# Pauses behind GpSimd's gathers: two small scratch writes behind each, of a width set per layer, in place of one behind every second

## The chip, the core and the metric

The kernel runs on one core of a Trainium2 chip. A core has five engines with a queue of instructions each: TensorE (PE in the profile; its weight loads are listed apart as PEld), VectorE (DVE), ScalarE (ACT), GpSimd (POOL) and SyncE (SP), which only issues DMAs. Sixteen DMA engines move data between device memory and the on-chip memories. The metric is the device time of one execution in microseconds (us), lower is better. Three timed runs of the kernel before took 1542.4 to 1545.57 us, with a median of 1544.14 us.

## What is computed

Four graph-attention layers run one after the other over 4096 nodes with 256 features, each as `x = x + layer(relu(layernorm(x)))`. Cut to one head, a layer does:

```python
h = x @ W
s_i, s_j = h @ a1, h @ a2
e = leaky_relu(s_i[:, None] + s_j[None, :], 0.2)
e = where(adj > 0, e, -very_large)
out = softmax(e, axis=1) @ h          # layers 1 and 3: elu of it
```

Layers 0 and 1 have one head; layer 2 has four heads of 64 features; layer 3 forms the softmax of `e` and that of `-e`, both over the same mask. The adjacency matrix `adj` is the same 4096 x 4096 matrix in all layers. Its entry (i, j) is set with a probability that falls with both indices, like `0.0039 * w_i * w_j` with `w_i` proportional to `(1 + i) ** -0.5`: the first rows and columns are rather full, the rest is sparse.

## The kernel before

All of it is `list_layers`. (A dense version, `dense_layers`, stands behind a flag that is set when the lists described here would overflow; with these inputs it is not run.)

**Tiles.** The nodes make 32 tiles of 128. A target tile (whose rows of `x` are being made) is handled by a `Unit`. Dense units take four target tiles at once (512 columns) and go over all 32 source tiles, with features and masks streamed from device memory by SP in chunks of four tiles (`s_gs`, `s_ms`). Listed units take one target tile and go over the four first source tiles (kept on chip, `pre` and `mpre`) and then over a list of only those sources that have an edge into the tile. `DENSE` says how many blocks of four tiles are dense in each layer: 4, 2, 1 and 1; the tiles behind them are listed.

**Lists and gathers.** In layer 0 the kernel builds, for each listed tile, an index (`idx`) of its sources, by VectorE and PE (`list_sources`). Sources come in blocks of 128 rows. `SHARED[T]` blocks hold sources for the whole tile; they are gathered as `s_gg` tiles (six buffers; four in layer 0). `QUADS[T]` groups of four blocks hold sources for one quarter of the tile each; they are gathered as `s_gq` tiles of four parts (two buffers). One gather is one indirect DMA issued by GpSimd: it reads 128 row numbers from `idx` on chip and fetches the 128 rows from a table in device memory (`table`, or `table_own` for the last block in layer 0). The mask of a block is gathered once in layer 0 into `mlist` from `mask_t`, or lies beside the features in the table's row and is copied out of the gathered tile by ScalarE (L1084 and L1174). All gathers go through the helper `gather` (L530), so that in the profile each stands under L532.

By `QUADS` and `SHARED`, layer 0 has 36 + 64 gathers for tiles 16 to 31 and 77 for masks, 177 in all; layer 1 has 69 + 96 for tiles 8 to 31, 165; layers 2 and 3 have 80 + 128 each for tiles 4 to 31, 208.

**The pause.** `gather` counts its calls while the program is built. After every second one (`RUN`) it writes a scratch tile `pause` of 128 x 256 floats with a memset on GpSimd (L541). Nothing reads the tile.

**A step.** For one source block: VectorE forms `p = max(grow, c) * mask` from the target's row factors `grow`, the source's column factor `c` (which lies in the last column of the gathered row) and the mask (L1151; for quads L1107 and L1110; in layer 2 ScalarE does part of it by L1090 and VectorE finishes with L1160). PE multiplies `p` with the source's features into an accumulator (L1193; L1130 for quads; L1210 and L1228 in layer 2). When a unit ends, VectorE and ScalarE normalise and add to `x`, and the pair's rows for the next layer are projected by `node_rows` and `project` (PE L746 and L778) and written to the next layer's table by SP.

**Order.** The order of all work is a written-out plan. `run` goes through it and at each place p issues the fetch of step p (its gathers included), the preparation of step p - 2, the weights of step p - 3 and the matmuls of step p - 6 (`LEAD`), and then a bit of the work that waits in `posts` (unit ends and projections). In layers 1 to 3 the plan begins with some dense steps alone, then listed tiles and dense steps alternate (over 24, 14 and 26 of the tiles), and then come the listed tiles that are left. Layer 1 takes tiles 16 to 31 and then 8 to 15; layers 2 and 3 take tiles 8 to 31 and then 4 to 7. GpSimd's queue keeps the order of the plan (`manual_schedule`); the framework inserts the waits between engines. A gather waits until the last reader of its buffer is done and, in layers 1 to 3, until the rows that it may fetch have been written.

Of the kernel before, what the change touches and what calls it, by code (L numbers as in the profile page):

```python
# [18 lines left out]
P = 128  # L19
# [5 lines left out]
IT = IB // P  # L25
# [454 lines left out]
FRONT = tuple(MW * ((l, False) in MASKS_IN.values()) for l in range(4))  # L480
TW = tuple(FRONT[l] + GW[l] + MW * ((l, True) in MASKS_IN.values()) for l in range(4))
LEAD = (0, 2, 3, 6)
RUN = 2
OWN0 = 7
HW = MW // 2
TURNS = (4, 5, 6, 1, 7, 2, 3)
# [3 lines left out]
def list_layers(ctx: ExitStack, tc: tile.TileContext, a: dict, out: bass.AP, flag):  # L490

    nc = tc.nc
# [32 lines left out]


    pause = const.tile([P, 256], F32, name="pause")
    gathers = [0]

    def gather(dst, src, index_ap, offset):  # L530

        nc.gpsimd.indirect_dma_start(  # L532
            out=dst,
            out_offset=None,
            in_=src,
            in_offset=bass.IndirectOffsetOnAxis(ap=index_ap, axis=0),
            element_offset=offset,
        )
        gathers[0] += 1
        if gathers[0] % RUN == 0:  # L540
            nc.gpsimd.memset(pause, 0.0)  # L541

    x = keep.tile([P, NT, D], F32, name="x")
    mpre = keep.tile([P, DP, N], U8, name="mpre")
    mlist = keep.tile([P, NLIST, P], U8, name="mlist")
# [3 lines left out]
    mask_t = {  # L549
        b: dram.tile([N + 1, IB], U8, name=f"mask_t{b}", tag=f"mask_t{b}")  # L550
        for b in range(NIB)
        if b not in MASKS_IN and b != OWN0
    }
# [139 lines left out]
    def pump(queue, n, width=1, force=False):  # L693

        k = 0
        while n and k < min(width, len(queue)):
            if queue[k][1] > clock[0] and not force:
                k += 1
                continue
            n -= 1  # L700
            try:
                queue[k][1] = clock[0] + (next(queue[k][0]) or 0.0)
            except StopIteration:
                queue.pop(k)

    def ensure(done):
        while not done():
            assert posts
            pump(posts, 1, force=True)
# [272 lines left out]
    index = {}  # L982
# [6 lines left out]
    def mask_slot(T, k):  # L989
        q = QUADS[T]  # L990
        if k >= GR * q:
            return OFFS[T] + k - GR * q, 0, P
        return OFFS[T] + SHARED[T] + k // GR, k % GR * GP, (k % GR + 1) * GP
# [3 lines left out]
    def gather_masks(n, tile=None):  # L997

        for T, k in list(masks_of):
            if not n or tile is None and T not in index:  # L1000
                break
            if tile in (None, T):
                slot, c0, c1 = mask_slot(T, k)
                gather(mlist[:, slot, c0:c1], mask_t[T // IT], index[T][:, k : k + 1], T % IT * P + c0)
                masks_of.remove((T, k))
                n -= 1

# [317 lines left out]
    def run(plan):  # L1325

        n = len(plan)
        for p in range(n + LEAD[3]):
            if p + 4 < n and plan[p + 4][1] == 0 and plan[p + 4][0].is_ready():
                plan[p + 4][0].prepare()  # L1330
            for lead, stage in zip(LEAD, (Unit.fetch, Unit.begin, Unit.weigh, Unit.multiply)):
                if 0 <= p - lead < n:
                    stage(*plan[p - lead])
            if p >= LEAD[3]:
                u = plan[p - LEAD[3]][0]
                clock[0] += u.cost
                pump(posts, u.rates[0], width=2)
                pump(lists_q, u.rates[1])
                gather_masks(u.rates[2])


    def listed_sources(L, T, pool):
        heads = list(range(L.H))
        l, n = L.l, L.part
        at, behind = MASKS_IN.get(T // IT, (-1, False))
        own = at == l
        more = 0 if not own else (T % IT + 1 if behind else IT - T % IT) * MW // IT
        source, first_col = L.table, FRONT[l]
        if T // IT == OWN0:
            at = 0  # L1350
            if l == 0:
                own, behind, source, first_col = True, T % IT >= IT // 2, table_own, HW
                more = (T % IT + 1 - IT // 2 if behind else IT // 2 - T % IT) * MW // IT
        front = 0 if behind else more
        width = GW[l] + more
        c0 = width * 4 - P if behind else 0

        def gather_rows(dst, k):
            gather(dst, source, index[T][:, k : k + 1], first_col - front)

        def get(i):
            if i < DP:
                g = L.g[:, i, :] if l == 0 else L.pre[:, i, :]
                m = mpre[:, i, T * P : (T + 1) * P]
                return heads, [g[:, h * n : (h + 1) * n] for h in heads], m
            ensure(lambda: all(L.ready))
            while T not in index:
                pump(lists_q, 1, force=True)
            if at < 0:
                gather_masks(CAPS[T], T)  # L1370
            k = i - DP
            m = mlist[:, OFFS[T] + k, :]
            if k < SHARED[T]:
                wide = pool.tile([P, width], F32, name=f"s_gg_{l}_{T}_{k}", tag="gg")
                gather_rows(wide, GR * QUADS[T] + k)
                if own:
                    kept, m = m, wide.bitcast(U8)[:, c0 : c0 + P]
                    copies[l, T, i] = kept, m
                g = wide[:, front : front + GW[l]]
                return heads, [g[:, h * n : (h + 1) * n] for h in heads], m  # L1380
            q = k - SHARED[T]
            wide = pool.tile([P, GR, width], F32, name=f"s_gq_{l}_{T}_{q}", tag="gq", bufs=2)
            for a in range(GR):
                gather_rows(wide[:, a, :], q * GR + a)
            if own:
                first = wide.bitcast(U8)[:, :, c0 : c0 + GP]
                rows_at, groups_at, bytes_at = (list(d) for d in first.ap)
                groups_at[0] += GP
                quad_masks[l, T, i] = m.rearrange("p (a i) -> p a i", a=GR), bass.AP(first.tensor, first.offset, [rows_at, groups_at, bytes_at])
            return heads, wide[:, :, front : front + GW[l]], m  # L1390

        return get
# [272 lines left out]
def gat_layers(tc: tile.TileContext, a: dict, out: bass.AP):  # L1665
    nc = tc.nc
    with tc.tile_pool(name="flag", bufs=1) as pool:
        flag = pool.tile([1, 1], I32, name="flag")

        with tc.manual_schedule(engines={mybir.EngineType.Pool}):  # L1670
            list_layers(tc, a, out, flag)
        again = nc.values_load(flag[0:1, 0:1], min_val=0, max_val=1)
        with tc.If(again > 0):
            dense_layers(tc, a, out)
# [45 lines left out]
```

## Time and profile before

| | |
|---|---|
| median of three timed runs | 1544.14 us |
| the profiled execution | 1640.54 us |
| its span, from first to last instruction | 1638.8 us |
| PE busy (matmuls) | 1445.7 us, 88% |
| DVE busy | 1182.5 us, 72% |
| POOL busy | 1037.6 us, 63% |
| ACT busy | 497.3 us, 30% |
| gathers into `s_gq`, 400 | 431.8 us, 1080 ns each |
| gathers into `s_gg`, 258 | 277.2 us, 1074 ns each |
| gathers into `mlist`, 77 | 91.1 us, 1183 ns each |
| `pause`, 379 | 132.3 us, 349 ns each |

The profiled execution is slower than the timed ones because it is recorded; it shows where time goes, not how much a run takes. A row of the groups view reads: line, engine, operation, written tile <- read tiles, shape, count | busy time in us, mean ns of one | idle time of the engine just before, with what ended it. The busy time of a group is the time in which at least one of its instructions ran, so overlapping ones count once. In the windows view each row is a stretch of the span: for each engine the busy time and the number of instructions, then the TensorE clock that was granted (1 is full), the share of time in which the DMA engines were busy, and the traffic. A row of the timeline has start, duration and the idle time in front of the instruction. In the chain of waits each row is a piece of the path that ended last: its start, its length, and the engine, tile and line, or "DMA" with the tiles for the time from a transfer's issue to its landing; "issue" is time for which the profile shows no reason.

### The profile page before, as it was taken

How to read it: one execution, taken by the hardware profiler on the slowest of the kernel's cores; microseconds unless marked ns; L12 is line 12 of the kernel's file. 1: busy time of each engine (PE TensorE's matmuls, PEld its weight loads, DVE VectorE, ACT ScalarE, POOL GpSimd, SP SyncE). 2: the span in 40 equal slices, each digit the busy share in tenths (PEclk: the TensorE clock that was granted, in tenths of full speed). 3: DMA queues.
4: the chain of work that ended last, by engine and by line, in shares of the span. 5: the costliest groups of instructions: out<-in, count | busy, mean ns of one | idle time of the engine just before them, and what ended most of it. 6: DMA issues, size and time to landing. Idle time of an engine off the chain costs nothing.

```text
span 1638.8 us, 30153 instructions
## 1 busy us (share of the span) xinstructions
PE 1445.7 (88%) x10558; PEld 1084.8 (66%) x10558; DVE 1182.5 (72%) x3424; ACT 497.3 (30%) x1569; POOL 1037.6 (63%) x1255
## 2 busy tenths in 40 slices
PE   6999898888888988888989889987877999899995
PEld 4887676666676866666645545566655877688873
DVE  6889989887677467655778879876755466577754
ACT  5631020011112023222335545565744111111111
POOL 9825888883513477767337776555556277867775
PEclk9999999999897999998999999989877999999997
DMA  7899999876414454554323333333333477766665
GB/s 261 283 320 297 320 299 293 223 201 161 115 33 145 112 152 126 141 154 133 114 73 107 97 105 97 106 90 99 91 102 106 131 217 209 217 193 198 205 184 146
DMA packets 161024, 272.72 MB, mean 166 GB/s; under 512 B 29664, under 2 KB 86462, under 8 KB 160862
## 3 DMA queue, kind: packets, MB, share of 16 engines
q1 hardware_dynamic: 117322, 146.32, 28.6%
q0 software_dynamic: 42704, 123.84, 28.2%
q8 instruction: 86, 1.41, 0.4%
q14 instruction: 76, 0.62, 0.1%
q10 hardware_dynamic: 836, 0.53, 0.1%
HBM read 225.22 MB, written 45.39 MB: 165 GB/s over the span
## 4 chain that ended last, share of the span: by engine, by line
PE 49%; DVE 7%; issue 6%; POOL 4%; DMA 4%; ACT 2%; another core or an unknown queue 1%; DVEq 0%; POOLq 0%; ACTq 0%
PE s_acc L1193 26%; PE s_pj L778 6%; PE s_acch L1210 5%; PE s_accm L1228 5%; DVE s_p L1151 3%; POOL s_gq L532 3%; PE s_acc L1130 2%; PE s_sT L1036 2%; DMA s_gq<-table,idx 1%; DMA s_gg<-table,idx 1%; PE s_acch L1130 1%; PE s_tp L746 1%; POOL s_gg L532 1%; DVE s_p L1160 1%
## 5 line engine op out<-in xcount | busy, mean ns | idle before, releaser
L532 POOL DMA_INDIRECT s_gq<-table,idx x400 | 431.8, 1080 | 188.7 <-issue 83.2
L532 POOL DMA_INDIRECT s_gg<-table,idx x258 | 277.2, 1074 | 277.4 <-DVE first L943 55.2
L1193 PE MATMUL s_acc<-g,s_p 128*128 128x257 f32 x1152 | 294.4, 401 | 17.4 <-DVE s_p L1151 12.2
L1193 PEld LDWEIGHTS s_acc<-g,s_p 128*128 128x128 f32 x1152 | 221.0, 200 | 59.7 <-DVE s_p L1151 16.5
L1193 PE MATMUL s_acc<-s_gs,s_p 128*128 128x257 f32 x896 | 212.3, 388 | 1.1 <-issue 0.9
L1151 DVE SCALAR_TENSOR_TENSOR s_p<-s_grow,pre,mpre 128x128 f32<-128x128 f32 (+1 forms) x576 | 188.4, 367 | 28.8 <-PE s_acc L1193 16.3
L778 PE MATMUL s_pj<-s_w,s_hT 128*128 128x259 f32 (+3 forms) x640 | 184.9, 428 | 24.4 <-issue 9.8
L1151 DVE SCALAR_TENSOR_TENSOR s_p<-s_grow,s_gs,s_ms 128x512 f32<-128x512 f32 x224 | 159.6, 748 | 56.5 <-PE s_acc L1193 20.1
L1193 PEld LDWEIGHTS s_acc<-s_gs,s_p 128*128 128x128 f32 x896 | 166.5, 192 | 39.0 <-issue 7.6
L1193 PE MATMUL s_acc<-pre,s_p 128*128 128x257 f32 x768 | 186.3, 391 | 3.2 <-issue 2.2
L1193 PEld LDWEIGHTS s_acc<-pre,s_p 128*128 128x128 f32 x768 | 147.2, 196 | 28.9 <-issue 4.3
L778 PEld LDWEIGHTS s_pj<-s_w,s_hT 128*128 128x128 f32 x640 | 126.2, 208 | 57.8 <-issue 14.4
L1193 PE MATMUL s_acc<-s_gg,s_p 128*128 128x257 f32 x530 | 137.9, 392 | 6.9 <-DVE s_p L1151 3.5
L1151 DVE SCALAR_TENSOR_TENSOR s_p<-s_grow,s_gg,mlist 128x128 f32<-128x128 f32 x363 | 116.5, 344 | 33.6 <-PE s_acc L1193 22.5
L541 POOL MEMSET pause<- 128x256 f32 x379 | 132.3, 349 | 0.2
L532 POOL DMA_INDIRECT mlist<-mask_t,idx x77 | 91.1, 1183 | 65.2 <-DVE idx L978 46.4
L1042 ACT ACTIVATE s_grow<-s_sT 128x256 f32<-128x256 f32 (+2 forms) x136 | 46.9, 368 | 257.4 <-PE s_sT L1036 136.5
L1107 DVE TENSOR_TENSOR s_p<-s_grow,s_gq 128x128 f32<-128x128 f32 (+1 forms) x168 | 52.4, 339 | 97.5 <-DMA s_gq<-table,idx 53.7
L1193 PEld LDWEIGHTS s_acc<-s_gg,s_p 128*128 128x128 f32 x530 | 100.2, 194 | 29.9 <-issue 8.5
L1210 PE MATMUL s_acch<-pre,s_p 128*64 128x65 f32 x1792 | 92.8, 237 | 28.9 <-issue 26.6
L1210 PEld LDWEIGHTS s_acch<-pre,s_p 128*64 128x64 f32 x1792 | 72.3, 144 | 67.0 <-issue 39.3
L1090 ACT ACTIVATE s_p<-s_grow,s_minus,pre 128x128 f32<-128x128 f32 x224 | 96.0, 485 | 62.0 <-PE s_accm L1228 25.7
(154 smaller groups left out, 2077.9 us busy)
## 6 DMA issues: line engine op xcount, KB each, us to landing
s_raw<-in_adjT SPq DMA_DIRECT2D x128, 512.0 KB
s_gs<-table SPq DMA_DIRECT2D x28, 516.0 KB
table<-s_g SPq DMA_DIRECT2D x28, 258.0 KB
mask_t<-s_m SPq DMA_DIRECT2D x28, 256.0 KB
s_ms<-mask_t SPq DMA_DIRECT2D x28, 256.0 KB
s_gq<-table,idx POOLq DMA_INDIRECT x400
table<-s_m SPq DMA_DIRECT2D x21, 256.0 KB
table<-g SPq DMA_DIRECT2D x8, 516.0 KB
```

The lines of the kernel that those rows point to most:

```text
L532: nc.gpsimd.indirect_dma_start(out=dst, out_offset=None, in_=src, in_offset=bass.IndirectOffsetOnAxis(ap=index_ap, axis=0), element_offset ...
L541: nc.gpsimd.memset(pause, 0.0)
L778: nc.tensor.matmul(ps, lhsT=hT[:, c, :], rhs=L.w[:, c, k * (D + 6) : k * (D + 6) + cols], start=(c == 0), stop=(c == 1),)
L1036: nc.tensor.transpose(ps[:, h - h0, it, :], L.s[:, T0 + it, h : h + 1].to_broadcast([P, P]), ident)
L1042: nc.scalar.activation(grow[:, h1:h2, :], ps[:, h1 - h0 : h2 - h0].rearrange("p h a b -> p h (a b)"), AF.Exp, scale=scale,)
L1090: nc.scalar.activation(w[:, h, :], u.grow[:, h, :], AF.Relu, scale=g[h][:, n - 1 : n], bias=minus)
L1107: nc.vector.tensor_tensor(p4[:, h0:h1], grow[:, h0:h1], c[:, h0:h1].to_broadcast([P, h1 - h0, GR, GP]), op=op)
L1130: nc.tensor.matmul(acc, lhsT=p[:, h, part], rhs=g[:, k, h * n : (h + 1) * n - 1], start=False, stop=last, skip_group_check=True,)
L1151: nc.vector.scalar_tensor_tensor(p[:, k, :], u.grow[:, h, :], g[k][:, n - 1 : n], m, op0=ALU.min if L.l == 3 and h == 1 else ALU.max, op1= ...
L1193: nc.tensor.matmul(u.accs[it][h], lhsT=p[:, k, it * P : (it + 1) * P], rhs=g[k][:, 0:n], start=first, stop=last, skip_group_check=u.quads > 0,
L1210: nc.tensor.matmul(u.accs[0][c : c + P // 2, h, :], lhsT=p[:, h, c : c + P // 2], rhs=g[h][:, 0 : DH + 1], start=first and h == 0, stop=la ...
L1228: nc.tensor.matmul(u.accs[h], lhsT=g[k][:, 0 : DH + 1], rhs=p[:, k, :], start=first, stop=last, skip_group_check=True,)
```

## The change

In place of one memset of 256 columns behind every second gather, two memsets stand behind each gather. Both write the same first columns of `pause`; how many is set by the layer of the gather: 176 in layer 0 (its mask gathers too), 144 in layer 1, 256 in layer 2 and 144 in layer 3. `gather` gets the layer as an argument; the counter goes.

```diff
-RUN = 2
+PAUSES = (176, 144, 256, 144)
...
     pause = const.tile([P, 256], F32, name="pause")
-    gathers = [0]
-
-    def gather(dst, src, index_ap, offset):
+
+    def gather(l, dst, src, index_ap, offset):
 
         nc.gpsimd.indirect_dma_start(
...
-        gathers[0] += 1
-        if gathers[0] % RUN == 0:
-            nc.gpsimd.memset(pause, 0.0)
+        for _ in range(2):
+            nc.gpsimd.memset(pause[:, 0 : PAUSES[l]], 0.0)
...
-                gather(mlist[:, slot, c0:c1], mask_t[T // IT], index[T][:, k : k + 1], T % IT * P + c0)
+                gather(0, mlist[:, slot, c0:c1], mask_t[T // IT], index[T][:, k : k + 1], T % IT * P + c0)
...
-            gather(dst, source, index[T][:, k : k + 1], first_col - front)
+            gather(l, dst, source, index[T][:, k : k + 1], first_col - front)
```

## The prediction

> **What bounds the kernel now.** First the cores, then the windows by layer (cut where the tiles' names change layer), the groups with shapes kept apart, POOL's timeline, the chain of waits in order of time. The profiled execution took 1640.54 us (span 1638.8 us and 1.7 us around it); the timed runs have a median of 1544.14 us, 0.94 of it. Sums below are made in profiled time and then multiplied by 0.94. One core runs, so there is no die to compare.
>
> ```profile
> core 0: us, PE busy (x) PEld busy (x) DVE busy (x) ACT busy (x) POOL busy (x), PEclk, DMA share, GB/s
> 0.00:475.00 475.00, 414.20 (x2286) 332.75 (x2287) 392.62 (x992) 113.68 (x413) 321.14 (x383) 0.96 0.81 242
> 475.00:805.00 330.00, 290.90 (x1573) 229.90 (x1572) 204.53 (x618) 82.00 (x293) 193.74 (x248) 0.93 0.47 131
> 805.00:1275.00 470.00, 406.48 (x4827) 256.91 (x4829) 355.79 (x1102) 249.28 (x726) 275.03 (x312) 0.90 0.35 96
> 1275.00:1639.00 364.00, 334.13 (x1884) 265.23 (x1880) 229.53 (x716) 52.33 (x138) 247.64 (x312) 0.97 0.66 190
> ```
>
> PE leads in every layer (86 to 92%). POOL is at 59 to 68%, so on average it is no bound. The chain says otherwise for some stretches; at the end of layer 2:
>
> ```profile
> 1265.29 0.95 POOL s_gq L532
> 1266.24 0.30 issue
> 1266.55 0.95 POOL s_gq L532
> 1267.50 0.00 issue
> 1267.50 0.33 POOL pause L541
> 1267.82 0.17 issue
> 1267.99 1.12 POOL s_gq L532
> 1269.11 0.31 issue
> 1269.42 3.18 DMA s_gq<-table,idx
> ```
>
> Here gathers stand one behind the other on the chain that ends last, each pause too, and the last one's landing (3.18 us from its start) is waited for. Going through the chain piece by piece I count 84 gathers on it: 3 in layer 0, 19 in layer 1, 21 in layer 2, 41 in layer 3. They sit at 685 to 732, 1195 to 1268, 1375 to 1394 and 1583 to 1622 us: where dense work to hide behind has run out, or where heavy tiles (8 or 9 gathers each) come.
>
> **What the skill says.** "Perfetto Trace Analysis", GPSIMD Engine Instruction: the reported span of a GpSimd instruction is unreliable, time them by start-to-start spacing. I do. "SBUF — State Buffer", Who interferes with whom: a VectorE instruction with two SBUF inputs contends with a GpSimd instruction that reads SBUF, not with one that only writes. The trace fits: gathers (which read an index) take 0.95 us at the median but up to 5.02 us, at 908.57 us beside an unbroken run of L1151 steps; the pause has a median of 0.33 us. "TensorE: Matmul & The Clock Gate", Part 1: PE's clock halves after an idle window and needs about 3.4 us of work to come back. The trace fits by its granted clock, 0.937 over the span, 0.90 in layer 2, where PE stalls most.
>
> **The change part by part.** It takes away 379 memsets of 256 columns (one behind every second gather) and a counter that exists only at build time. It adds 2 x 758 = 1516 memsets. By the lists in the code the layers have 177, 165, 208 and 208 gathers (the groups add to the same 758). No DMA, wait or buffer is added or moved.
>
> ```profile
> L541 POOL MEMSET pause<- 128x256 f32 x379 | 132.3, 349 | 0.2
> L507 POOL MEMSET s_ones<- 128x128 f32 x1 | 0.2, 194 | 0.0
> L524 POOL MEMSET places<- 128x1 f32 x28 | 1.0, 98 | 0.0
> ```
>
> ```profile
> 1299.24 1.00 POOL L532 DMA_INDIRECT s_gg<-table,idx  x1 [0.30 <-issue]
> 1300.24 0.33 POOL L541 MEMSET pause<- 128x256 f32 x1
> 1300.73 0.95 POOL L532 DMA_INDIRECT s_gg<-table,idx  x1 [0.17 <-issue]
> 1301.98 0.95 POOL L532 DMA_INDIRECT s_gg<-table,idx  x1 [0.30 <-issue]
> 1302.93 0.33 POOL L541 MEMSET pause<- 128x256 f32 x1
> ```
>
> *Before.* From one gather's end to the next one's start: 0.30 us without a pause, 0.33 + 0.16 = 0.49 us with one. Mean 0.395 us.
>
> *Width.* 128 columns show 194 ns, 256 show 325 ns (the minimum): 1.02 ns a column, 63 ns fixed. So 144, 176 and 256 columns are 210, 243 and 325 ns.
>
> *Two in a row.* The trace has no such pair of this size. The 28 one-column memsets show 98 ns each but fill 1.0 us together, 36 ns each: they overlap by 62 ns. Lower bound of a pair: twice the span less 62 ns; upper bound: twice the span. I take the lower one, as those memsets overlapped throughout.
>
> *After.* Pair plus 0.16 us: 0.52 us at 144, 0.59 at 176, 0.75 at 256 (upper: 0.58, 0.65, 0.81). Added per gather: 0.19 us in layer 0, 0.125 in layers 1 and 3, 0.355 in layer 2. Over all gathers: 34 + 21 + 74 + 26 = 155 us more of POOL (upper 202). No layer comes over 80% of POOL, so most is hidden: by POOL's waits for a free buffer, behind PE's work.
>
> *On the path.* (1) The 84 gathers on the chain: 3 x 0.19 + 19 x 0.125 + 21 x 0.355 + 41 x 0.125 = 15.5 us. (2) Two stretches where POOL's own waits no longer cover it. Counting in POOL's timeline, 712 to 797 us has 55 gathers and 5.7 us of waits against 6.9 us added, and 1298 to 1375 us has 51 gathers and 3.6 us against 6.4 us: 1.2 + 2.8 = 4 us at most, of which I take 3. (3) Layer 0, 140 to 300 us: 98 gathers without one wait, so POOL falls 98 x 0.19 = 18.6 us further behind; from 300 to 460 us it waits 37 us, which takes most of it back. I put 4 us on the path; bounds 0 and 18.6. (4) A gift: a gather held by a VectorE run ends with that run, whenever it was issued. Beyond 0.95 us each (758 x 0.95 = 720 of the groups' 826 us) the gathers spend 106 us, so held; a pause that falls inside is free. I take 4 us off (about a fifth of 1 to 3). Sum: 15.5 + 3 + 4 - 4 = 18.5 us profiled, 17 us timed: 1544 + 17 = 1561, and I say 1560.
>
> *Who is queued behind.* Behind a memset on POOL stand only later gathers (L732 and L736 of layer 0 ended at 92 us, before the first gather). For these wait ScalarE's mask copies (L1084, L1174) and VectorE's L1107, then PE: the copies hold ScalarE's in-order queue, so the next `s_grow` is late too. Late next is the free `s_gq` buffer (two of them), which POOL itself waits for.
>
> **Rivals.** *Faster: layer 0 is short of DMA.* From 140 to 300 us the DMA engines are 97% busy, with the adjacency stream and 98 gathers; slower gathers leave the stream more of it, and their own traffic moves to a stretch at 65%. Price: at most PE's idle time there, 160 - 141.6 = 18 us. It decides if it gives more than the 15 us that the chain costs; then, with the chain's cost half absorbed in held gathers, 1544 - 18 + 7 = 1533. For: the share. Against: VectorE waits only some 5 us for that stream (L1472) from 140 to 460 us. *No change: all is hidden.* POOL idles 600 us of the span; 1544. Against: 84 gathers on the chain. *Much slower: pairs do not overlap and POOL becomes the bound.* Chain 21 us, layer 0 half of 98 x 0.25 = 12, stretches 6, and 8 for PE work at half clock behind stalls grown by some 16 us: 47 x 0.94 = 44, so 1588. For: layer 2's granted clock is already 0.90. *The change doesn't do what it says*: if the second memset, which repeats the first, were dropped on the way to the chip, the gaps would be 0.37 to 0.49 us, close to the 0.395 us of now, and the time with them; this joins the no-change case.
>
> **How the numbers follow.** My forecast 42% (its own range 1550 to 1572), faster by the first rival 37% (1526 to 1540), no change 8%, much slower 13% (1573 to 1595). That gives faster 0.37, same 0.08, slower 0.55; 0.2% is about what a measurement of this kernel can tell from no change. The range 1531 to 1577 leaves out a quarter of the faster case (9%) and most of the last (9%).
>
> **What would show it.** Right: pauses x1516 with spans near 0.21, 0.24 and 0.33 us; gather end to next start 0.52, 0.59, 0.75 us; POOL near 72% busy; more POOL pieces on the chain at the ends of layers 1, 2 and 3; layer 2 longer by some 9 us, layer 3 by some 7. Wrong: layers 1 to 3 no longer than before although the gaps have grown (gathers on the chain are then not what sets the end), or layer 0 shorter with fewer waits for `s_raw`.

## The result: 1792 us in place of 1543, sixteen per cent slower

| | before | after |
|---|---|---|
| timed runs, median | 1543.27 us (1539.48 to 1545.57) | 1791.95 us (1786.01 to 1795.24) |
| ratio of the medians | | 1.161, 95% interval 1.158 to 1.165 |
| profiled execution | 1640.54 us | 1790.98 us |

The forecast was 1560 us with a range of 1531 to 1577. The time lies 215 us above the range, and beyond the worst rival (1588) too. Times here and below are medians of all executions; ratios are taken over fast executions alone (within 1.5% of a kernel's fastest).

One sentence ahead of the prediction has to be put right first. The profiled execution of before (1640.54 us) was not slow because it was recorded: a later recording of the same kernel took 1549 us (run 1). Where the text below compares traces, it uses that recording, called "before, second recording".

The groups view of the changed kernel, GpSimd's memsets by shape (columns: busy us, mean ns of one | idle time ahead of them):

```profile
L539 POOL MEMSET pause<- 128x144 f32 x746 | 169.4, 227 | 21.6
L539 POOL MEMSET pause<- 128x256 f32 x416 | 133.3, 320 | 12.1
L539 POOL MEMSET pause<- 128x176 f32 x354 | 103.5, 292 | 10.3
```

746 + 416 + 354 is 1516, and the durations are near those of the width line (210, 325 and 243 ns). New is the last column: 44 us of idle time directly ahead of memsets, where before had 0.2. The second memset of a pair does not follow at once.

GpSimd's timeline in layer 3 of the changed kernel (start, duration, line and tile; in brackets the idle time in front and its releaser; a pair of memsets is one row):

```profile
1501.21 0.51 POOL L539 MEMSET pause<- 128x144 f32 x2
1502.21 0.95 POOL L531 DMA_INDIRECT s_gg<-table,idx  x1 [0.49 <-PE s_acc L1191]
1503.17 0.51 POOL L539 MEMSET pause<- 128x144 f32 x2
...
1507.12 0.51 POOL L539 MEMSET pause<- 128x144 f32 x2
1507.78 1.14 POOL L531 DMA_INDIRECT s_gq<-table,idx  x1 [0.16 <-issue]
```

A pair of 144 columns takes 0.51 us, more than twice 0.227. Behind it the next gather starts after 0.16 us, as assumed, or after 0.49 us. (The bracket names PE as what ended the 0.49 us; run 18 below speaks against that.) So from one gather's end to the next one's start it is 0.66 or 1.0 us here, where the prediction had 0.52, and at most 0.58.

The chain of waits, its sum by engine, of the changed kernel:

```profile
PE 40%; POOL 29%; DMA 14%; DVE 8%; issue 7%; ACT 1%; DVEq 0%; POOLq 0%; SPq 0%; ACTq 0%
```

and of before, second recording:

```profile
PE 42%; DVE 11%; POOL 7%; DMA 6%; issue 3%; ACT 2%; POOLq 0%; DVEq 0%; ACTq 0%
```

(The chain of before can be followed back to 442 us only, so its shares add up to less. In the profile that the prediction read, GpSimd and DMA had 4% each.) The chain in order of time, in layer 2 of the changed kernel, shows how the new pieces follow each other:

```profile
1186.38 0.33 POOL pause L539
1186.71 0.04 issue
1186.75 0.02 POOLq L531
1186.77 0.31 POOL pause L539
1187.08 0.39 issue
1187.47 0.95 POOL s_gg L531
```

From 1186.38 to 1187.47 this one pause costs 1.09 us of the path: two memsets, 0.06 us between them, and 0.39 us for which the chain names no reason. POOLq is a piece of GpSimd's queue: here a separate semaphore instruction of the next gather, 0.04 us behind the end of the first memset.

Who waits now: the largest row of the waits view, first of the changed kernel (us in total, times, longest us),

```profile
DVE s_p L1105 <- DMA s_gq<-table,idx: 299.3, 78, 9.2
```

and the same row of before, second recording:

```profile
DVE s_p L1107 <- DMA s_gq<-table,idx: 82.8, 31, 7.0
```

VectorE waits 216 us longer for gathered quads, and PE waits behind VectorE (for `s_p` at L1108, before L1110: 105 us in place of 18).

The windows by layer, cut at the first gather of each layer: the changed kernel,

```profile
0.00:564.00 564.00, 464.70 (x2535) 370.57 (x2536) 417.57 (x1080) 123.98 (x449) 383.15 (x649) 0.90 0.72 209
564.00:929.00 365.00, 301.90 (x1429) 225.54 (x1429) 203.87 (x603) 81.29 (x297) 242.25 (x495) 0.90 0.41 114
929.00:1397.00 468.00, 378.25 (x4838) 247.66 (x4837) 338.67 (x1057) 245.71 (x700) 362.52 (x625) 0.87 0.36 98
1397.00:1790.00 393.00, 326.68 (x1761) 252.88 (x1760) 207.35 (x686) 46.68 (x123) 303.75 (x624) 0.92 0.60 171
```

and before, second recording:

```profile
0.00:517.00 517.00, 450.64 (x2544) 362.13 (x2545) 417.49 (x1080) 124.05 (x449) 331.18 (x384) 0.93 0.77 228
517.00:824.00 307.00, 285.14 (x1421) 216.12 (x1421) 206.86 (x603) 82.69 (x297) 193.33 (x248) 0.96 0.49 136
824.00:1217.00 393.00, 350.65 (x4833) 232.95 (x4832) 335.10 (x1055) 244.86 (x700) 299.27 (x312) 0.95 0.42 116
1217.00:1548.00 331.00, 307.46 (x1766) 243.86 (x1764) 217.02 (x688) 47.77 (x123) 245.68 (x312) 0.97 0.70 203
```

Every layer is longer, by 47, 58, 75 and 62 us. VectorE's work is the same in each (417 and 417 us, 204 and 207, 339 and 335, 207 and 217). The granted clock is lower in each, 0.87 to 0.92 against 0.93 to 0.97. PE is busy for 82% of the span in place of 90%. The lower clock agrees with what the Trainium skill, "TensorE: Matmul & The Clock Gate", Part 1, says (the clock halves after an idle window), and goes with the longer busy time of PE in layers 0 to 3 (14, 17, 28 and 19 us).

GpSimd's account, added up from the two traces between the first and the last gather of each layer. "Gaps" are the times from one gather's end to the next one's start where they are under 1.3 us; "waits" are those of 1.3 us or more; for 21 of 22 of them in before, and for 10 of 23 in the changed kernel, the trace names another engine as what ended them:

| us, before (second recording) -> after | gathers run | gaps | waits | sum |
|---|---|---|---|---|
| layer 0 | 214 -> 198 | 73 -> 138 | 28 -> 37 | 316 -> 373 |
| layer 1 | 166 -> 167 | 64 -> 124 | 32 -> 31 | 263 -> 322 |
| layer 2 | 265 -> 229 | 84 -> 202 | 14 -> 8 | 363 -> 439 |
| layer 3 | 212 -> 210 | 79 -> 160 | 23 -> 7 | 314 -> 378 |
| sum | 857 -> 805 | 300 -> 625 | 98 -> 82 | 1256 -> 1512 |

The sums grow by 256 us, the span by 242. The gaps grew by 325 us, not 155. Gathers that are spaced out run 53 us shorter, and the waits gave back only 16 us.

### The profile page after: what moved, and what is told of

The parts are those of the page before. It is cut to its first block, busy times and chain, and to the rows that moved or that the text cites. A ratio compares the mean times of both kernels' runs of the same rounds, so it can differ in the third digit from the quotient of the medians.

```text
span 1789.2 us, 31281 instructions
## 1 busy us (share of the span) xinstructions
PE 1471.5 (82%) x10558; PEld 1096.7 (61%) x10558; DVE 1167.5 (65%) x3424; ACT 497.7 (28%) x1569; POOL 1291.7 (72%) x2392
## 4 chain that ended last, share of the span: by engine, by line
PE 40%; POOL 29%; DMA 14%; DVE 8%; issue 7%; ACT 1%; DVEq 0%; POOLq 0%; SPq 0%; ACTq 0%
PE s_acc L1191 20%; POOL s_gq L531 13%; DMA s_gq<-table,idx 9%; POOL pause L539 9%; PE s_pj L776 6%; PE s_accm L1226 4%; POOL s_gg L531 4%; PE s_acch L1208 3%; DMA s_gg<-table,idx 2%; PE s_acc L1128 2%; DVE s_p L1149 2%; POOL mlist L531 2%; PE idx_ps L966 1%; PE s_tp L744 1%; DVE s_p L1105 1%
## 5 line engine op out<-in xcount | busy, mean ns | idle before, releaser
L531 POOL DMA_INDIRECT s_gq<-table,idx x400 | 424.9, 1062 | 91.2 <-issue 71.3
L531 POOL DMA_INDIRECT s_gg<-table,idx x258 | 267.1, 1035 | 249.3 <-issue 58.7
L539 POOL MEMSET pause<- 128x144 f32 (+2 forms) x1516 | 406.2, 268 | 44.0
L1191 PE MATMUL s_acc<-g,s_p 128*128 128x257 f32 x1152 | 308.7, 416 | 15.6 <-DVE s_p L1149 15.1
L1191 PEld LDWEIGHTS s_acc<-g,s_p 128*128 128x128 f32 x1152 | 230.7, 208 | 62.1 <-DVE s_p L1149 21.9
L1191 PE MATMUL s_acc<-s_gs,s_p 128*128 128x257 f32 x896 | 231.1, 412 | 4.7 <-DVE s_p L1149 4.5
L1191 PEld LDWEIGHTS s_acc<-s_gs,s_p 128*128 128x128 f32 x896 | 179.2, 206 | 52.3 <-DVE s_p L1149 20.7
L1149 DVE SCALAR_TENSOR_TENSOR s_p<-s_grow,pre,mpre 128x128 f32<-128x128 f32 (+1 forms) x576 | 182.2, 363 | 12.7 <-PE s_acc L1191 9.8
L1149 DVE SCALAR_TENSOR_TENSOR s_p<-s_grow,s_gs,s_ms 128x512 f32<-128x512 f32 x224 | 157.3, 744 | 24.1 <-PE s_acc L1191 19.8
L1128 PE MATMUL s_acc<-s_gq,s_p 128*32 128x257 f32 x832 | 72.0, 448 | 105.3 <-DVE s_p L1108 105.3
L1149 DVE SCALAR_TENSOR_TENSOR s_p<-s_grow,s_gg,mlist 128x128 f32<-128x128 f32 x363 | 116.2, 341 | 51.1 <-DMA s_gg<-table,idx 33.1
L1226 PE MATMUL s_accm<-s_p,s_gs 128*65 128x512 f32 x224 | 111.7, 652 | 0.7 <-DVE s_p L1149 0.7
```

The costliest lines, as they stand in the source:

```text
L531: nc.gpsimd.indirect_dma_start(out=dst, out_offset=None, in_=src, in_offset=bass.IndirectOffsetOnAxis(ap=index_ap, axis=0), element_offset ...
L539: nc.gpsimd.memset(pause[:, 0 : PAUSES[l]], 0.0)
L1128: nc.tensor.matmul(acc, lhsT=p[:, h, part], rhs=g[:, k, h * n : (h + 1) * n - 1], start=False, stop=last, skip_group_check=True,)
L1149: nc.vector.scalar_tensor_tensor(p[:, k, :], u.grow[:, h, :], g[k][:, n - 1 : n], m, op0=ALU.min if L.l == 3 and h == 1 else ALU.max, op1= ...
L1191: nc.tensor.matmul(u.accs[it][h], lhsT=p[:, k, it * P : (it + 1) * P], rhs=g[k][:, 0:n], start=first, stop=last, skip_group_check=u.quads > 0,
L1226: nc.tensor.matmul(u.accs[h], lhsT=g[k][:, 0 : DH + 1], rhs=p[:, k, :], start=first, stop=last, skip_group_check=True,)
```

## Experiments

Theory A: the time follows GpSimd's cycle from gather to gather, since its waits hold little slack. Theory D: of the pair's price, most is that the second memset waits for the first (it writes the same columns), which holds GpSimd's queue so that a gather with several waits is set up late. Rivals: the written columns themselves disturb VectorE (E), pauses give something back (C), two instructions in a row are dear whether they wait or not (F).

Diffs are against the changed kernel, that of run 2 against the kernel before. The runs fell on several chips. On some the kernel before takes 1544 us, on others 1650 or 1675 us. A ratio is always to before on the same chip.

| run | what stands behind each gather | before there, us | time, us | ratio, 95% interval |
|---|---|---|---|---|
| 1 | as before | 1544.37 | 1546.08 | 1.0007 (0.9989 to 1.0026) |
| 2 | nothing | 1544.37 | 1522.55 | 0.986 (0.982 to 0.990) |
| 3 | pair of one column | 1544.37 | 1659.13 | 1.074 (1.070 to 1.078) |
| 4 | one memset of 288 or 340 columns | 1544.37 | 1599.72 | 1.035 (1.031 to 1.039) |
| 5 | pair apart in layers 0, 1, 3 | 1675.11 | 1680.66 | 1.002 (0.999 to 1.005) |
| 6 | the change in layer 0 alone | 1675.11 | 1713.62 | 1.021 (1.014 to 1.028) |
| 7 | the change in layer 2 alone | 1675.11 | 1677.47 | 1.001 (0.999 to 1.004) |
| 8 | one memset of one column | 1675.11 | 1727.56 | 1.027 (1.020 to 1.034) |
| 9 | the change | 1650.2 | 1791.61 | 1.083 (1.075 to 1.090) |
| 10 | as 5 | 1650.2 | 1680.28 | 1.016 (1.009 to 1.023) |
| 11 | as 8 | 1650.2 | 1703.15 | 1.025 (1.013 to 1.036) |
| 12 | nothing | 1650.2 | 1696.63 | 1.027 (1.019 to 1.034) |
| 13 | as 6 | 1544.35 | 1600.12 | 1.037 (1.031 to 1.042) |
| 14 | as 7 | 1544.35 | 1617.57 | 1.047 (1.041 to 1.053) |
| 15 | as 4 | 1544.35 | 1599.42 | 1.036 (1.031 to 1.041) |
| 16 | as 3 | 1544.35 | 1659.51 | 1.075 (1.070 to 1.080) |
| 17 | the change | 1543.57 | 1790.51 | 1.159 (1.155 to 1.164) |
| 18 | as 5 | 1543.57 | 1679.36 | 1.088 (1.084 to 1.092) |

**Run 1, the kernel before, unchanged.**

> The kernel before, unchanged. Its profiled execution on record took 1640 us and its timed runs 1543 us, while the changed kernel's profiled execution (1791 us) is as long as its timed runs (1792 us). If recording costs 6% of this kernel, the profiled execution is again near 1640 us. If the one on record was an unlucky execution, it is near 1545 us, and the profile I predicted from showed stalls that the timed runs do not have. Timed: 1543 us, ratio 1.00.

Its profiled execution took 1549 us. Recording costs nothing that shows, so the profile that I predicted from came from an execution 6% slower than the timed ones. How it differed is in the waits of PE. The largest row in that first profile of before:

```profile
PE s_acch L1210 <- issue: 33.2, 76, 1.2
```

PE stops 76 times between the short matmuls of layer 2, for nothing that the profile shows. No such row is in the second recording. It is in run 12's trace, on the chip where before takes 1650 us:

```profile
PE s_acch L1208 <- issue: 32.2, 58, 1.7
```

It is also in runs 6, 8 and 11 (27 to 37 us), on chips of this kind, and in none of runs 2, 13, 17 and 18, where before takes 1544 us. So the first profile probably came from a chip of the slower kind; that is inferred from this row and from its time, not shown. What it meant for the forecast can be counted: GpSimd's waits of 1.3 us or more were 38, 52, 114 and 31 us in the four layers there, 236 us, and are 98 us in the second recording. The cover of layer 2 was 114 us in the profile and is 14 us where the timed runs were made.

**Run 2, no pause.**

```diff
-        if gathers[0] % RUN == 0:
-            nc.gpsimd.memset(pause, 0.0)
```

> No pause at all: the gathers follow each other directly, 0.30 us from end to next start in place of a mean 0.395 us, so GpSimd has some 72 us less to do. Theory A (the time follows GpSimd's gather cycle): 1500 to 1540 us, faster than before. Theory B (GpSimd had slack before, and only what exceeds a threshold counts): 1543 us, within 0.5%. Rival C (pauses give something back, to the DMA streams or to VectorE): slower than before, 1560 us or more.

1522.55 us, as theory A has it, and against B and C. Gaps fall by 80 us to 220, the time by 22: here waits take up most of the difference (98 to 188 us).

**Runs 3 and 16, the pair with one column.**

```diff
-PAUSES = (176, 144, 256, 144)
+PAUSES = (1, 1, 1, 1)
```

> The changed kernel with both memsets one column wide (about 0.1 us each) in place of 144 to 256 columns; number, order and waits stay. From the widths alone the pause between gathers is shorter by 0.31, 0.25, 0.44 and 0.25 us in layers 0 to 3, some 240 us of GpSimd in all. Theory A (length of the gather cycle, whatever makes it up): 1560 to 1620 us. Theory D (the second memset waits for the first, and a gather that has several waits is set up only after it; the columns matter little): over 1700 us. Rival E (the written columns themselves disturb VectorE): 1543 us, with DVE instruction means as before.

> The pair of one-column memsets behind each gather, once more. Where the kernel before takes 1544 us: 1653 to 1662 us, as at first. Where it takes 1650 us or more: theory A says slack covers most of it, 0 to 1.5% slower than before; theory D's part that a third of the gathers are set up late shows again as gaps near 0.9 us in either case.

1659 us twice. Almost nothing is written, yet the kernel is 7.4% slower than before, so E falls: of the added 247 us, 115 remain. Nor do VectorE's instructions run shorter: those that form `s_p` from `pre` (L1149) have a mean of 365 ns in run 16, 363 in the changed kernel and 364 in before, second recording. The timeline of GpSimd in run 16:

```profile
1501.38 0.27 POOL L539 MEMSET pause<- 128x1 f32 x2
1501.80 0.94 POOL L531 DMA_INDIRECT s_gg<-table,idx  x1
1502.74 0.27 POOL L539 MEMSET pause<- 128x1 f32 x2
1503.64 1.40 POOL L531 DMA_INDIRECT s_gq<-table,idx  x1 [0.63 <-PE s_acc L1191]
```

Two memsets of 0.1 us fill 0.27 us, and the gather behind them comes after 0.14 or after 0.63 us. The time lies above A's range and below D's 1700: neither had all of it. Gaps add up to 437 us in run 16. That is only 23 us more than in run 15 below, for 60 us more time, so the sum of the gaps does not give the time by itself; where the rest comes from was not found.

**Runs 4 and 15, one wide memset.**

```diff
-    pause = const.tile([P, 256], F32, name="pause")
+    pause = const.tile([P, 340], F32, name="pause")
...
-        for _ in range(2):
-            nc.gpsimd.memset(pause[:, 0 : PAUSES[l]], 0.0)
+        nc.gpsimd.memset(pause[:, 0 : min(2 * PAUSES[l], 340)], 0.0)
```

> One memset behind each gather in place of the pair, of 340, 288, 340 and 288 columns in layers 0 to 3 (nearly the pair's columns, but in layer 2, where it would be 512). No second memset waits for a first. By the width line 0.41 and 0.36 us long, with the next gather 0.16 us behind it as before: 0.57 and 0.52 us between gathers against 0.66 to 1.17 us with the pair and 0.395 us before. Theory A (length of the cycle): 1600 to 1680 us. Theory D (the pair's chained wait and the late set-up behind it are the cost): under 1580 us. Rival E (columns written): in layers 0, 1 and 3 as slow as the changed kernel, 1730 us or more.

> One wide memset behind each gather, once more. Where the kernel before takes 1544 us: 1597 to 1603 us, as at first. Where it takes 1650 us or more: theory A alone (gaps of 414 us in all are less than the 510 us of the pair without the inner wait, which cost 0 to 1.6%): within 1% of before. If the time falls with longer pauses until GpSimd is the bound: faster than before, by 0.5 to 2%.

1600 us twice. In layers 0, 1 and 3 it writes what the pair writes (340 of 352 columns in layer 0; in layer 2 it is 340 in place of 512), with a gap of 0.52 us in layers 1 and 3 and mostly 0.56 in layer 0, and E falls again. (The wider tile was not tried by itself.) The time is just below A's range (1600 to 1680); D's "under 1580" was too low. So both count: the pause's length, and a further part that only the pair has.

**Runs 5, 10 and 18, the pair on columns apart.**

```diff
-    pause = const.tile([P, 256], F32, name="pause")
+    pause = const.tile([P, 340], F32, name="pause")
...
-        for _ in range(2):
-            nc.gpsimd.memset(pause[:, 0 : PAUSES[l]], 0.0)
+        w = min(PAUSES[l], 170) if l != 2 else 256
+        for c in (0, 340 - w):
+            nc.gpsimd.memset(pause[:, c : c + w], 0.0)
```

In layers 0, 1 and 3 the two memsets share no column; in layer 2 they overlap and wait as in the change.

> The changed kernel with the two memsets of a pair on columns that do not overlap (0 to 170 and 170 to 340 in layer 0; 0 to 144 and 196 to 340 in layers 1 and 3), so that the second does not wait for the first; layer 2 stays as in the changed kernel. Theory D (the second memset's wait holds GpSimd's queue, so that a gather with several waits is set up late): between gathers 0.60 to 0.62 us in layers 0, 1 and 3, few gaps over 0.8 us, 92 us of gaps less in layers 0, 1 and 3 together than in the changed kernel: 1690 to 1720 us. Rival F (it is that two short instructions stand there, waiting or not): only the 0.06 us between the two goes, and a third of the gaps stay near 1 us: 1750 to 1770 us.

> The changed kernel with the two memsets of a pair on columns that do not overlap, in layers 0, 1 and 3, once more, now beside the changed kernel. Its gaps were 0.65, 0.56 and 0.56 us on average in those layers (0.84, 0.79 and 0.79 with the pair that waits). Theory A with D: on a chip with a 1544 us kernel before, 1690 to 1720 us; on one with 1675 us, 1675 to 1690 us again. Rival F (the waits in the pair do not matter): as the changed kernel.

> The pair on columns that do not overlap in layers 0, 1 and 3, layer 2 as in the changed kernel. Where the kernel before takes 1544 us, theory A (GpSimd's gaps count in full once its waits are used up): its gaps are some 511 us in all against 300 us before and 625 us in the changed kernel, so 1675 to 1690 us, as on the other chips. Rival F: as the changed kernel, 1760 us or more.

1680 us on all three chips, below the 1690 to 1720 us that D had for run 5. The first comparison (1.002) fell on a chip with a slow kernel before and says nothing on F alone; runs 9 and 10, and 17 and 18, stand beside each other and do: 111 us of the change's 141 or 247 us go with the wait inside the pair, and F falls. GpSimd's timeline in run 18, layer 3:

```profile
1501.25 0.39 POOL L540 MEMSET pause<- 128x144 f32 x2
1501.80 0.95 POOL L531 DMA_INDIRECT s_gq<-table,idx  x1 [0.16 <-issue]
1502.76 0.39 POOL L540 MEMSET pause<- 128x144 f32 x2
1503.31 0.95 POOL L531 DMA_INDIRECT s_gg<-table,idx  x1 [0.16 <-issue]
```

The pair takes 0.39 us in place of 0.51: the second memset now starts 0.075 us before the first ends. The gather behind it, an `s_gg` gather too, comes 0.16 us later. In run 17 I sorted the gathers that start less than 0.8 us behind a pair by whether a separate semaphore instruction of theirs (they wait for several engines) stands in the trace between the gather ahead and it: 476 without one start after 0.156 us at the median, 265 with one after 0.487 us. In run 15, with a single memset, the two kinds start after 0.165 us alike. Run 18 has both cases in one trace: those with such an instruction start after 0.161 or 0.162 us in layers 0, 1 and 3, and after 0.479 us in layer 2, where the pair still waits. So it takes both, a pair with a wait in it and a gather with a separate semaphore instruction, and no wait for PE is needed for it: such a wait would scatter, but in run 17 the gather stands 0.72 to 0.75 us behind that instruction in nearly every case.

What GpSimd's queue does in this time stays open. That such a gather is set up late because the queue is held, as D has it, is not shown: in run 17 its semaphore instruction is done between the two memsets, in run 15 only behind the single memset, and there the gather mostly follows 0.12 us later.

265 x 0.33 = 88 us is the price of these late starts by themselves; 97 of the 265 are in layer 2, which run 18 leaves as it is. From run 17 to run 18 the gaps fall by 113 us (624 to 511), the time by 111. By these figures about half of that is late starts (168 x 0.33 = 55 us) and half the overlap (550 pairs x 0.12 = 66 us), an estimate.

**Runs 6 and 13, layer 0 alone; runs 7 and 14, layer 2 alone.**

```diff
+    gathers = [0]
...
-        for _ in range(2):
-            nc.gpsimd.memset(pause[:, 0 : PAUSES[l]], 0.0)
+        gathers[0] += 1
+        if l == 0:
+            for _ in range(2):
+                nc.gpsimd.memset(pause[:, 0 : PAUSES[l]], 0.0)
+        elif gathers[0] % 2 == 0:
+            nc.gpsimd.memset(pause, 0.0)
```

(`l == 2` in runs 7 and 14.)

> The pair behind each gather in layer 0 alone; layers 1 to 3 as before. Theory A (GpSimd's cycle sets the time in every layer): the gathers of layer 0 take 57 us longer in the changed kernel's trace than in the kernel before: 1580 to 1600 us. My prediction's step 3 (mostly absorbed by GpSimd's waits after 300 us): 1543 to 1550 us. Rival (layer 0 is set by the adjacency stream, and slower gathers leave more to it): under 1543 us.

> The pair behind each gather in layer 0 alone, once more. Where the kernel before takes 1544 us: theory A 1580 to 1600 us, my prediction's step 3 1543 to 1550 us. Where it takes 1650 us or more: 2 to 2.5% slower, as at first.

> The pair behind each gather in layer 2 alone; layers 0, 1 and 3 as before. Theory A: the gathers of layer 2 span 76 us more in the changed kernel's trace than in the kernel before: 1610 to 1625 us. My prediction's step 1 (only the gathers at the layer's end count): 1550 to 1553 us. In between if what layer 2 loses is partly found again at the start of layer 3.

> The pair behind each gather in layer 2 alone, once more. Where the kernel before takes 1544 us, GpSimd waits only 14 us in layer 2 in gaps over 1.3 us: theory A 1610 to 1625 us, my prediction's step 1 1550 to 1553 us. Where it takes 1650 us or more, it waits there some 130 us, which covers the 119 us of longer gaps: within 0.5% of before, as at first.

Where before takes 1544 us, layer 0 alone costs 55.8 us and layer 2 alone 73.2 us, the first 0.1 us above theory A's range (1580 to 1600 us in all), the second inside its own. Together that is 129 of the 247 us; the rest, 118 us, is left for layers 1 and 3, whose gathers span 59 + 63 = 122 us more in the table above. Where before takes 1675 us, layer 0 costs 38.5 us and layer 2 nothing: run 6's trace, with before's pauses in layer 2, has 134 us of waits there, run 7's only 15, with 126 us more of gaps. There the pause is paid out of waits. PE's short stops among the matmuls of layer 2 (run 1) are gone with it, too: 33.5 us in run 6, 0.5 in run 7.

In layer 0 the prediction counted GpSimd's later waits as cover. GpSimd's timeline has the largest of them, in before (second recording),

```profile
416.11 1.81 POOL L532 DMA_INDIRECT s_gg<-table_own,idx  x1 [20.47 <-DVE s_z L732]
```

and in run 13:

```profile
467.98 1.81 POOL L532 DMA_INDIRECT s_gg<-table_own,idx  x1 [18.94 <-DVE s_z L735]
```

The gather comes 52 us later, and its wait is only 1.5 us shorter. The bracket names `s_z`, which ended just ahead of the start, but the gather does not use it. By the code the gather reads the index list `idx` of its own target tile, and VectorE finished writing that (L978; L981 in run 13) 0.27 us ahead of the start in both traces, and in the first profile of before. By the code, VectorE makes the lists piece by piece between the steps of layer 0, so they are late when the steps are. Such a wait moves with the delay; it is not slack.

**Runs 8 and 11, one memset of one column.**

```diff
-        for _ in range(2):
-            nc.gpsimd.memset(pause[:, 0 : PAUSES[l]], 0.0)
+        nc.gpsimd.memset(pause[:, 0 : 1], 0.0)
```

> One memset of one column behind each gather. Without any memset the next gather starts 0.305 us after the last one's end; behind a single memset it starts 0.16 us after the memset's end. Theory G (the set-up of the next gather runs while the memset runs): 0.10 + 0.16 = 0.26 us between gathers, 34 us of GpSimd less than with none, at the 0.42 us of time for each us of gap that the kernels with no pause and before show: 1505 to 1512 us, faster than the 1522 us with none. Rival H (the memset holds the queue as in the pair, and a third of the gathers are set up late): 0.4 us or more on average, 1545 to 1590 us.

> One memset of one column behind each gather, once more, now beside no memset at all. Its gap was 0.305 us, the same as with none, so neither theory G (0.26 us) nor H (0.4 us) held; the memset fits in the 0.305 us that a gather needs anyway. So the two must now be equal: on a chip with a 1544 us kernel before, 1518 to 1527 us; on one with 1675 us, 1715 to 1735 us again. If they differ, the memset does something besides its time.

Both G and H fell by the gap: it is 0.305 us, as with no memset. Their times were meant for a chip where before takes 1544 us, and this kernel was not run on one. Run 11 (1703.15 us) and run 12 (1696.63 us, no memset) agree within their intervals, though 1703 is below the 1715 to 1735 us given. A memset of 0.1 us costs nothing that shows in a gap of 0.305 us.

**Runs 9, 12 and 17, the change and no pause, on other chips.**

> The changed kernel, unchanged, beside the kernel before on one chip. On a chip where the kernel before takes 1544 us: 1785 to 1800 us again, ratio 1.16. On a chip where it takes 1675 us, as in the last four runs, GpSimd waits there 257 us for others in the gaps over 1.3 us (in the trace of the kernel with the change in layer 0 alone, layers 1 to 3: 227 us, against 70 us on the first chip), so theory A, slack first and then one for one, gives much less: 1750 to 1800 us, ratio 1.04 to 1.07.

> No pause at all, once more. On a chip with a 1544 us kernel before: 1515 to 1530 us. On a chip with a 1675 us kernel before: theory A says never slower than before, 1640 to 1675 us; the run with one tiny memset says 1715 to 1735 us there, slower than before by 2.7%, so that pauses give something back on such a chip.

> The changed kernel, unchanged. Where the kernel before takes 1544 us, as where it takes 1650 us: 1787 to 1797 us, since GpSimd's queue sets its time on any chip.

The change takes 1791.61 and 1790.51 us where before takes 1650 and 1544 us: its time is the same on each chip, which fits A, with GpSimd as the bound (the ratio on the slower chip, 1.083, is above the 1.04 to 1.07 that I gave). But A fell for the kernel without pauses: there it is 2.7% slower than before, where on the other chip it is 1.4% faster. On such a chip something gets better when gathers are spaced, until GpSimd is the bound. What that is was not found. Nothing that was tried beats before on both kinds of chip; having no pause beats it on one.

## Why the prediction was wrong, step by step

Two terms failed. The longer gaps were put at 155 us and measured 325; and an eighth of them (18.5 us) was taken to reach the time, where the time grew by 249 us, about three quarters of the 325.

- **Width** held: 227, 292 and 320 ns measured for 210, 243 and 325; only 176 columns, in layer 0, were much longer in the mean (258 ns at the median). The line is made of reported spans, though the prediction says that it times by start-to-start spacing.
- **Two in a row** failed. I took the lower bound because the 28 one-column memsets overlapped, and called twice the span the upper one. Those 28 write a column each and do not wait for each other; the pair does, since both write the same columns. The true value lies above my upper bound: 0.51 us for 144 columns (0.36 to 0.42 said). The Trainium skill, "GPSIMD Engine Reference", Instruction dispatch, says that an instruction's completion holds back what waits on its semaphore, not the next instruction as such. The traces agree: 0.39 us for a pair without that wait, 0.51 us with it. I had asked how long the instruction is, and not what it waits for.
- **After: pair plus 0.16 us** failed for a third of the gathers. 0.16 us was right for those without a separate semaphore instruction (0.156). Those with one came after 0.49 us, which happens only behind a pair that waits; why is not shown. Mean gaps became 0.84, 0.79, 0.99 and 0.79 us in layers 0 to 3, in place of 0.59, 0.52, 0.75 and 0.52. The term "155 us more of GpSimd (upper 202)" measured 325 us.
- **"No layer comes over 80% of POOL, so most is hidden"** failed, and would have failed with right gaps too. In run 18 gaps grew by 211 us (300 to 511) and the time by 136; in run 4 by 113 and 55. So about half to two thirds of what is added counts, and by that my 155 us would have cost some 75 to 100 us, not 17. That is an estimate from these two pairs. The share of busy time was the wrong measure, for the gap ahead of a gather is not busy, and neither are waits that move along.
- **On the path, (1) the 84 gathers on the chain**, 15.5 us in all: the count takes in 22 pieces of GpSimd's queue and leaves out 15 gathers that the chain shows by their landing; 77 would be right and changes the sum by 1 us. What failed is that their number was taken to stay. In the changed kernel 367 of the 758 gathers stand on the chain, counted so, with 113 in the second recording, and GpSimd has 29% of it in place of 7%. Layer 2 had 7.5 us of this sum and cost 73 us.
- **(2) two stretches**, 3 us in all: my working counted stretches with few waits in a profile that had more than twice the waits of the timed executions.
- **(3) layer 0**, 4 us (bounds 0 to 18.6), measured 55.8 us: the later waits did not take it back, since the largest of them moves with the delay.
- **(4) the gift** was real: gathers run 53 us shorter in sum, against 325 us of longer gaps, a sixth. The prediction took off about a fifth (4 of 22.5 us), so its share was about right.
- **The factor 0.94** from profiled to timed time had no meaning; the two executions differed in their stalls, not by a constant.
- **The rivals.** *Faster* and *no change* fell: layer 0 became longer, not shorter, though VectorE's waits for the adjacency stream did fall, from 13 to 10 us in the changed kernel. *Much slower* named the right mechanism (the pairs do not overlap and GpSimd becomes the bound), at 13%; its price of 44 us was low for the reasons above: it charged the chain and a few stretches, while every layer grew by nearly what its gathers span more (47, 58, 75 and 62 us for 57, 59, 76 and 64).
- **What would show it.** GpSimd's 72% busy is as forecast, by luck: its busy time (1292 us) and the span (1789 us) both came out larger. It shows how little that number says here.

## What to carry to other kernels

Before pricing an instruction that is put twice in a row, ask whether the second depends on the first: here the wait in the middle cost 111 us of 247 in three of the four layers, by the lost overlap and by the later start of those gathers behind it that have a separate semaphore instruction. Count an engine's waits as slack only if what is waited for doesn't depend on the same engine's earlier work. And look whether the profile's own time fits the timed runs before its stalls are taken as cover.

## What was not expected of the hardware

One program takes 1544 us on some chips and 1650 or 1675 us on others, and the order of two variants turns round with it: without pauses 0.986 of before on one, 1.027 on another. The kernels with the longest gaps take the same on all (1791 us on two chips, 1680 us for the pair apart on three). Without a pause no gap between two gathers was under 0.303 us, and most were 0.305 (runs 2 and 12); a one-column memset fits into it unseen (runs 8 and 11). A wait inside a pair of memsets delays the gather behind it by 0.33 us, but only where that gather has a separate semaphore instruction (run 17; run 18, layer 2).
